# Softmax sums of a dilated attention kernel: the [112, 4, 12] tile of sums and reciprocals moves from SBUF to the PSUM bank of the scores

## The chip, the cores and the metric

The kernel runs on one core of one Trainium2 chip. The metric is device time in microseconds (us) of one execution. Three runs of the kernel before gave 5148.28, 5153.74 and 5155.06 us; their median, 5153.74 us, is the time that the change is compared with.

## What is computed

The input x has shape (16, 56, 56, 384) in float32: 16 images of 56 x 56 pixels with 384 channels. Two layers are applied, each as x + f(group_norm(x)) with 32 groups of 12 channels. The first f is an attention over the 3 x 3 neighbours of each pixel, for three groups of 128 channels with dilations 1, 2 and 3, and 4 heads of 32 channels in each. The second is a 3 x 3 depthwise convolution with weights clipped and replaced by their sign. Cut to what matters:

```python
qkv = einsum('bchw,oc->bohw', group_norm(x), w_qkv)     # 3 x 384 outputs
for each dilation group, head and pixel:
    attn = einsum('bgdn,bgdkn->bgnk', q, k_of_9_neighbours) * 32 ** -0.5
    attn = softmax(attn, axis=-1)                       # over the 9 neighbours
    out  = einsum('bgnk,bgdkn->bgnd', attn, v_of_9_neighbours)
x = x + einsum('bhwc,oc->bhwo', out, w_proj) + b_proj
x = x + depthwise_conv3x3(group_norm(x), sign(clip(w_conv)))
```

The change sits in the softmax: in the sums over the nine neighbours, their reciprocals and the product with them.

## The kernel before, in words

The work is cut into strips of 8 image rows (448 pixels); an image has 7 of them, so there are 112, which are numbered 0 to 111 here. Channels lie on the partitions, pixels along the free dimension. Three plans put the pieces of a strip at due times: `plan_a` brings the input in, transposes it (`turn`, L435) and takes statistics (L448); `plan_b` does the attention; `plan_c` does the second normalisation (L721, L789), the convolution (L752, L762 to L768 for two of the three channel groups; L818, L825 and L831 to L834 for the third) and the transposes back for the output (L841). `plan_b` starts a strip every 9 steps, and `plan_c` handles the strip of ten strips earlier, so that some sixteen strips are in flight.

The attention of one strip goes like this.

- `k_or_v` and `query` project the normalised input with matmuls (L476) into PSUM tiles `pkv` and `pq`. ScalarE copies k and v to SBUF (L486).
- `score` multiplies `pq` with k shifted to three neighbours at a time, on VectorE (L529, nine instructions of 1344 elements for each strip).
- `score_rounds` sums the products over the 32 channels of each head with matmuls (L514) into one PSUM tile `ps`, which collects all 27 pairs of group and neighbour. They are issued in three bursts of 8, 8 and 11 matmuls, the first after the third L529 of its strip.
- `softmax_1` copies `ps` to SBUF (ScalarE, L544), transposes it so that pixels lie on 112 partitions (L547, tile `pt_s`), takes the maximum over the neighbours (L550, tile `mx`), subtracts it (L551) and applies the exponential (ScalarE, L552). The weights are in the SBUF tile `ew`, 4 x 108 elements on 112 partitions.
- `softmax_2` sums the weights over the neighbours (L556), takes the reciprocals (L557) and multiplies (L558), all on VectorE. The tile in between, `sm`, holds 48 elements on each partition.
- `softmax_3` to `softmax_5` split the weights into three bf16 terms (ScalarE L566, GpSimd L570, L574, L575), and a DMA transposes them (L580).
- `weigh` spreads the weights over the channels with small matmuls (L593, tile `pb_a`), multiplies them with v on VectorE (L600) and adds up on GpSimd (L608, 1344 elements; L611 and L612).
- `out_project` projects (L626, tile `po`) and adds bias and residual (L629).

What sets the order: each piece is put at a step and, within a step, at a rank (`at(when, order, piece)`); sorted by these, the pieces give the program order. In step 9m + 10 of strip m `softmax_2` comes first. The first score burst of strip m + 1 is due at step 9m + 11. A scheduler then orders the instructions of each engine by its own estimates of cost, and puts in the waits on semaphores. [...]

Tiles come from pools. A pool with n buffers for a tag gives a buffer to the next tile of that tag when every instruction that used the tile before has finished. [...]`ps_mt` has three (most matmul outputs), `ps_q` one, `ps_bc` three in one tile (`pb_a`), and `ps_s` has the last, with a single tile tag "s" and one buffer. Before the change only `ps` (L508) used it. `sm` shares the tag "mx" with `mx` in the SBUF pool `s_p`, also with one buffer.

The kernel before has these three places around the change:

```python
had["ps"] = ps_s.tile([P, 512], F32, tag="s", name="ps")          # L508
at(t0 + 10, SOFTMAX, softmax_2)                                    # L648
at(t0 + i, BURST, lambda i=i: score_rounds(3 if i == 8 else 2))    # L646
```

Of the kernel before, what the change touches and what calls it, by code (L numbers as in the profile page):

```python
# [8 lines left out]
F32 = mybir.dt.float32  # L9
# [8 lines left out]
P = 128  # L18
# [6 lines left out]
SUB = 112  # L25
# [10 lines left out]
def dilated_attention_then_binary_conv(  # L36
# [32 lines left out]
    NSUB = PX // SUB  # L69
# [17 lines left out]
    ps_s = ctx.enter_context(tc.tile_pool(name="ps_s", bufs=1, space=PSUM))  # L87
# [67 lines left out]
    s_p = ctx.enter_context(tc.tile_pool(name="s_p", bufs=1))  # L155
# [302 lines left out]
    def plan_b(m, t0):  # L458
# [73 lines left out]
        GH = NG * HEADS  # L532
        weights = ew.rearrange("p (s v) -> p s v", s=NSUB)[:, :, :NR]

        def by_neighbour(ap):
            return ap.rearrange("p s (o k) -> p s o k", o=NTAP)

        def over_neighbours(ap):
            return ap.unsqueeze(2).to_broadcast([SUB, NSUB, NTAP, GH])
# [12 lines left out]
            nc.scalar.activation(weights, weights, AF.Exp, scale=SCALE)  # L552

        def softmax_2():
            sm = s_p.tile([SUB, NSUB, GH], F32, tag="mx", name="sm")
            nc.vector.reduce_sum(sm, by_neighbour(weights).rearrange("p s o k -> p s k o"), axis=AX.X)  # L556
            nc.vector.reciprocal(sm, sm)  # L557
            nc.vector.tensor_tensor(by_neighbour(weights), by_neighbour(weights), over_neighbours(sm), ALU.mult)  # L558
# [84 lines left out]
        for i in range(9):  # L643
            at(t0 + i, SCORE, lambda i=i: score(i))
            if i % 3 == 2:
                at(t0 + i, BURST, lambda i=i: score_rounds(3 if i == 8 else 2))  # L646
        at(t0 + 9, SOFTMAX, softmax_1)
        at(t0 + 10, SOFTMAX, softmax_2)  # L648
        at(t0 + 11, SOFTMAX, softmax_3)
        at(t0 + 11, SOFTMAX, softmax_4)  # L650
# [318 lines left out]
```

## Time and profile before

| what | value |
|---|---|
| median of three runs | 5153.74 us |
| the profiled execution's own time | 5160.07 us |
| its span, first to last instruction | 5157.9 us |
| mean granted TensorE clock | 0.979 |
| TensorE (PE) busy | 96% |
| VectorE (DVE) busy | 87% |
| GpSimd (POOL) busy | 82% |
| ScalarE (ACT) busy | 48% |
| DMA over the span | 162 GB/s mean |
| instructions | 72661 |

How to read it: the page and the answers of the trace come from one execution, which took 5160.07 us, 0.12% more than the median of the runs. In a list of groups each line has the line of the kernel, the engine, the operation, output and inputs, the shape, the count, then busy time in us, mean duration in ns, and the idle time of the engine just before with what ended it. In a timeline each line has the start in us from the beginning of the span, the duration in us, engine, line and operation; a bracket at the end gives the idle time before it and what ended it. A float32 matmul shows as two records, so a burst of 8 matmuls is "x16". The clock column PEclk is the share of full TensorE clock that was granted.

### The profile page before, as it was taken

How to read it: one execution, taken by the hardware profiler on the slowest of the kernel's cores; microseconds unless marked ns; L12 is line 12 of the kernel's file. 1: busy time of each engine (PE TensorE's matmuls, PEld its weight loads, DVE VectorE, ACT ScalarE, POOL GpSimd, SP SyncE). 2: the span in 40 equal slices, each digit the busy share in tenths (PEclk: the TensorE clock that was granted, in tenths of full speed). 3: DMA queues.
4: the chain of work that ended last, by engine and by line, in shares of the span. 5: the costliest groups of instructions: out<-in, count | busy, mean ns of one | idle time of the engine just before them, and what ended most of it. 6: DMA issues, size and time to landing. Idle time of an engine off the chain costs nothing. (4 is left out here: it accounts for less than half of the span.)

```text
span 5157.9 us, 72661 instructions
## 1 busy us (share of the span) xinstructions
PE 4967.5 (96%) x25093; PEld 2259.1 (44%) x25093; DVE 4475.9 (87%) x4575; ACT 2478.8 (48%) x4365; POOL 4248.0 (82%) x2998
## 2 busy tenths in 40 slices
PE   7999999999999999999999999999999999999975
PEld 4444444444444444444444444444444444444422
DVE  4888888888898888898888898888889988888876
ACT  3223545555454555545545554554555545444445
POOL 2778888888888888889888888888889888888891
PEclk8999999999999999999999999999999999999986
DMA  6443666666566665666666666666656656555455
GB/s 194 125 123 112 171 170 175 171 168 172 166 172 167 169 169 167 172 163 172 170 175 169 168 174 169 168 168 167 173 164 174 168 166 170 146 135 139 119 144 162
DMA packets 813957, 836.45 MB, mean 162 GB/s; under 512 B 362643, under 2 KB 782870, under 8 KB 813590
## 3 DMA queue, kind: packets, MB, share of 16 engines
q1 hardware_dynamic: 805606, 819.81, 57.8%
q10 hardware_dynamic: 7984, 12.00, 0.7%
q8 instruction: 199, 3.26, 0.3%
q14 instruction: 168, 1.38, 0.1%
HBM read 477.43 MB, written 231.21 MB: 137 GB/s over the span
## 5 line engine op out<-in xcount | busy, mean ns | idle before, releaser
L608 POOL TENSOR_TENSOR w<-w 128x1344 f32<-128x1344 f32 x672 | 2049.5, 3050 | 300.8 <-DVE w L600 262.3
L600 DVE TENSOR_TENSOR w<-pb_a,v 128x1344 f32<-128x1344 f32 x1008 | 1561.6, 1549 | 132.5 <-PE pb_a L593 102.1
L529 DVE TENSOR_TENSOR t<-pq,k 128x1344 f32<-128x1344 f32 x1008 | 1527.6, 1547 | 130.0 <-PE pq L476 128.8
L476 PE MATMUL pkv<-xn,wqkvT 128*128 128x448 f32 x3924 | 1553.3, 545 | 26.7 <-ACT xa L447 26.2
L476 PEld LDWEIGHTS pkv<-xn,wqkvT 128*128 128x128 f32 x3924 | 727.6, 191 | 706.4 <-issue 631.6
L476 PE MATMUL pq<-xn,wqkvT 128*128 128x448 f32 x1962 | 862.4, 567 | 0.0
L626 PE MATMUL po<-y,wprojT 128*128 128x448 f32 x2016 | 836.2, 551 | 20.1 <-POOL y L612 17.3
L721 ACT ACTIVATE z<-z,mrz 96x448 f32<-96x448 f32 x840 | 580.4, 752 | 262.6 <-DMA z<-x1d 220.6
L825 POOL TENSOR_TENSOR m<-m 128x1344 f32<-128x1344 f32 x210 | 640.0, 3047 | 68.6 <-ACT m L818 62.6
L514 PE MATMUL ps<-t,sel 128*32 128x448 f32 x6048 | 661.1, 546 | 1.8 <-DVE t L529 1.7
L818 ACT ACTIVATE m<-zg,ktap 128x448 f32<-128x448 f32 x945 | 568.9, 659 | 17.6 <-POOL m L825 8.5
L626 PEld LDWEIGHTS po<-y,wprojT 128*128 128x128 f32 x2016 | 375.8, 191 | 378.8 <-issue 346.2
L486 ACT COPY v<-pkv 128x448 f32<-128x448 f32 x336 | 178.5, 531 | 755.2 <-PE pkv L476 755.1
L476 PEld LDWEIGHTS pq<-xn,wqkvT 128*128 128x128 f32 x1962 | 339.4, 190 | 349.9 <-issue 349.9
L593 PE MATMUL pb_a<-aT,spread 24*128 24x448 bf16 x3024 | 370.4, 360 | 52.6 <-DVE w L600 48.4
L629 DVE SCALAR_TENSOR_TENSOR xr<-po,bias,xr 128x448 f32<-128x448 f32 x336 | 227.5, 677 | 210.7 <-PE po L626 205.8
L612 POOL TENSOR_TENSOR y<-y,w 128x448 f32<-128x448 f32 x336 | 381.7, 1136 | 20.3
L611 POOL TENSOR_TENSOR y<-w 128x448 f32<-128x448 f32 x336 | 382.3, 1138 | 17.3
L447 ACT COPY xa<-pt_x 128x448 f32<-128x448 f32 x315 | 167.4, 533 | 474.6 <-PE pt_x L435 469.2
L593 PEld LDWEIGHTS <-spread 24*128 24x128 bf16 x3024 | 102.5, 91 | 627.5 <-issue 608.6
L570 POOL TENSOR_TENSOR rest<-ew,e 112x512 f32<-112x512 f32 x112 | 130.2, 1163 | 292.5 <-ACT e L566 291.3
L752 PE MATMUL pc<-z,kdiag 96*32 96x440 f32 x3360 | 359.5, 546 | 8.8 <-POOL z L723 7.6
(141 smaller groups left out, 4745.8 us busy)
## 6 DMA issues: line engine op xcount, KB each, us to landing
z<-x1d SPq DMA_DIRECT2D x570, 224.0 KB, 3.8
xr<-xd SPq DMA_DIRECT2D x112, 672.0 KB, 4.3
x1d<-xr SPq DMA_DIRECT2D x112, 672.0 KB, 3.2
xn<-xd SPq DMA_DIRECT2D x109, 672.0 KB, 4.6
xin<-in_x_dram SPq DMA_DIRECT2D x105, 672.0 KB, 7.8
xd<-xa SPq DMA_DIRECT2D x315, 224.0 KB, 3.6
out_dram<-osb SPq DMA_DIRECT2D x420, 168.0 KB, 3.5
x<-x1d SPq DMA_DIRECT2D x80, 560.0 KB, 5.7
```

What stands on the lines that cost most here:

```text
L476: nc.tensor.matmul(dst[:, :PX], wqkvT[:, cc, o0 : o0 + P], had["xn"][:, cc, :], start=(cc == 0), stop=(cc == NG - 1))
L514: return nc.tensor.matmul(had["ps"][32 * j : 32 * j + 32, :PX], sel[:, s0 : s0 + 32], tk, start=(issued[j] == 1), stop=(issued[j] == len(r ...
L529: nc.vector.tensor_tensor(t.rearrange("p k (r w) -> p k r w", w=W), q3, k3, ALU.mult)
L593: return nc.tensor.matmul(pb[:, kx, :PX].rearrange("p (s n) -> p s n", s=NSUB), spread[rows_of, v % 2, :], had["a"][rows_of, :, v // 8, :] ...
L600: nc.vector.tensor_tensor(w.rearrange("p k (r w) -> p k r w", w=W), pb[:, :, :PX].rearrange("p k (r w) -> p k r w", w=W), three(kv[1][g][m ...
L608: nc.gpsimd.tensor_tensor(w0, w0, w, ALU.add)
L611: nc.gpsimd.tensor_tensor(y, w0[:, 0], w0[:, 1], ALU.add)
L612: nc.gpsimd.tensor_tensor(y, y, w0[:, 2], ALU.add)
L626: nc.tensor.matmul(po[:, :PX], wprojT[:, g, j * P : (j + 1) * P], had[f"y{g}"], start=(g == 0), stop=(g == NG - 1))
L721: nc.scalar.activation(z, z, AF.Identity, bias=mrz[:, j, q, 0:1], scale=mrz[:, j, q, 1:2])
L818: nc.scalar.activation(rows(t[:, kx]), zp[:, ky : ky + ROWS, kx : kx + W], AF.Copy, scale=ktap[:, JG, o : o + 1])
L825: nc.gpsimd.tensor_tensor(had["m"], had["m"], t, ALU.add)
```

## The change

In `softmax_2` the tile `sm` is no longer taken from the SBUF pool `s_p` (tag "mx") but from the PSUM pool `ps_s` with the tag "s", the one buffer that `ps` uses. The first 48 columns of 112 partitions of that bank hold the sums and then their reciprocals. The three VectorE instructions stay, with the same shapes; the sum now writes PSUM, the reciprocal reads and writes PSUM, and the product reads its second operand from PSUM. Every later line of the file moves down by one.

```diff
         def softmax_2():
-            sm = s_p.tile([SUB, NSUB, GH], F32, tag="mx", name="sm")
+            sm = ps_s.tile([P, 512], F32, tag="s", name="psm")[:SUB, : NSUB * GH]
+            sm = sm.rearrange("p (s k) -> p s k", s=NSUB)
             nc.vector.reduce_sum(sm, by_neighbour(weights).rearrange("p s o k -> p s k o"), axis=AX.X)
             nc.vector.reciprocal(sm, sm)
             nc.vector.tensor_tensor(by_neighbour(weights), by_neighbour(weights), over_neighbours(sm), ALU.mult)
```

In the built program the tag now passes from `ps` of strip m to `psm` of strip m and on to `ps` of strip m + 1. The order of instructions on each engine is the same for most of the span. On TensorE it differs in two stretches. For strips 3 to 9 one of the three L476 matmuls for `pq` that stood behind the first score burst stands ahead of it. In the last image, for most strips, the eight L752 matmuls that stood behind the first score burst stand ahead of it; with them a few L600, L762, L765 and L768 change places on VectorE.

## The prediction

> **What bounds the kernel now.** I read the page first, then the groups of VectorE by form, then the timeline around L558 in single strips, then the waits of TensorE by stretch.
>
> The page's first part:
>
> ```profile
> PE 4967.5 (96%) x25093; PEld 2259.1 (44%) x25093; DVE 4475.9 (87%) x4575; ACT 2478.8 (48%) x4365; POOL 4248.0 (82%) x2998
> ```
>
> TensorE sets the pace: in strips 10 to 99 one L558 follows another after 43.40 us again and again, and the matmuls follow each other without gaps. Whatever delays TensorE there lengthens the run one for one; VectorE time alone is worth nothing. So the question is where this change touches TensorE. The groups of VectorE by form (count, then busy us and mean ns) show the three instructions concerned and their nearest relatives:
>
> ```profile
> L558 DVE TENSOR_TENSOR ew<-ew,sm 112x432 f32<-112x432 f32 x112 | 118.2, 1055 | 3.7
> L556 DVE TENSOR_REDUCE sm<-ew 112x48 f32<-112x432 f32 x112 | 102.1, 911 | 0.2 <-ACT ew L552 0.2
> ...
> L551 DVE TENSOR_TENSOR ew<-pt_s,mx 112x432 f32<-112x432 f32 x112 | 65.9, 589 | 0.0
> L557 DVE RECIPROCAL sm<-sm 112x48 f32<-112x48 f32 x112 | 50.7, 452 | 3.7
> ```
>
> L558 and L551 do the same work on the same shape, yet L558 takes 1055 ns on average and L551 589. The tile view of `sm` gives L558 as 586/608/3077 ns (minimum, median, maximum): most are normal and some are stopped. The timeline of such a strip:
>
> ```profile
> 2363.94 0.91 DVE L556 TENSOR_REDUCE sm<-ew 112x48 f32<-112x432 f32 x1
> 2364.22 3.06 POOL L608 TENSOR_TENSOR w<-w 128x1344 f32<-128x1344 f32 x1
> ...
> 2364.89 0.45 DVE L557 RECIPROCAL sm<-sm 112x48 f32<-112x48 f32 x1
> ...
> 2365.38 2.38 DVE L558 TENSOR_TENSOR ew<-ew,sm 112x432 f32<-112x432 f32 x1
> ...
> 2365.97 1.71 PE L514 MATMUL ps<-t,sel 128*32 128x448 f32 x16
> ...
> 2369.80 0.37 PE L593 MATMUL pb_a<-aT,spread 24*128 24x448 bf16 x3 [0.64 <-DVE w L600]
> ```
>
> L558 (start 2365.38) ends at 2367.76, half a microsecond after GpSimd's L608 ends (2367.28). L556 and L557 run at normal length beside the same L608. L600, two instructions behind L558, is late, its bank is late, and TensorE stands still for 0.64 us before L593. In a strip where L608 is out of the way:
>
> ```profile
> 2539.17 0.45 DVE L557 RECIPROCAL sm<-sm 112x48 f32<-112x48 f32 x1
> ...
> 2539.66 0.61 DVE L558 TENSOR_TENSOR ew<-ew,sm 112x432 f32<-112x432 f32 x1
> ...
> 2540.25 1.71 PE L514 MATMUL ps<-t,sel 128*32 128x448 f32 x16
> ```
>
> L558 takes 0.61 us and ends at 2540.27. The score burst starts at 2540.25: free of L558 now, but at the same moment by chance. That coincidence matters below.
>
> [...]L558 has two SBUF inputs and stalls up to 3077 ns; L551 with one input in PSUM has a longest duration of 608 ns in 112.[...]
>
> **The change part by part.** I numbered the 112 instances of L558 in order of time and noted the TensorE gap after each.
>
> 1. [...]After the change L558 has one SBUF input, as L551 has, so I take all stalls away (0 to 100% is the range; it is a rival below). In strips 10 to 99 29 of 90 are stalled, 31.8 us together. A stall costs TensorE nothing up to an L558 of about 1.67 us, since L593 has 1.06 us of slack behind L600; beyond that one for one (1.96 us gives 0.29, 2.38 us gives 0.71). Only 15 strips pay, 8.8 us in all. That is 28% of the stall time; the rest was hidden behind the matmuls of L514 and L752 anyway. Gain: 8.8.
>
> 2. The last image (strips 100 to 110). VectorE is fuller there and nine L558 stall, by 13.6 us. The waits of TensorE in the window 4480 to 4940:
>
> ```profile
> PE pb_a L593 <- DVE w L600: 13.5, 9, 2.5
> ```
>
> After four of these waits the granted clock reads 0.50, for 3.4, 6.8, 6.8 and 10.2 us (4530.2, 4574.6, 4707.7 and 4844.3 on), 27.2 us together, so 13.6 us of work are lost, about 2 of them inside the waits. The ceiling is 13.5 + 11.5 = 25 us. But strips 100 and 107, which do not stall, take 43.43 and 43.34 us to the next, as long as strips 103 and 104 that wait for 1.7 us (43.23 and 43.35): they wait 0.8 us at L626 for ScalarE's L486 instead. So most of a wait comes back. I credit 0.4 us for each of nine waits (3.6) and 70% of the clock loss (8): 12, with 3 to 22 as ends. In the new order L752 stands ahead of the burst (1.54 us of matmuls), which covers the new wait here.
>
> 3. Added: the wait of the first score burst for L558. Behind it on TensorE stand L752, L593 and all else of the strip; VectorE's L762 and L600 wait for those. A TensorE instruction that waits for VectorE starts 0.055 us after its end (the floor of L593 after L600 and of L514 after L529). In 78 of the 90 strips the burst starts 0.01 us before the end of an unstalled L558, so it moves by 0.065 us: 5.1 us. In the other 12 it starts 0.07 us after it: nothing. The 0.065 us repeats in each strip, since the chain L529 to L558 is itself started by TensorE (`pq`): no slack takes it up.
>
> 4. Strips 3 to 9: the burst started 0.80 us before the end of L558 (306.08 against 306.88). One L476 now stands ahead of it, two records 0.375 us apart, 0.75 us. What is left is 0.80 + 0.055 - 0.75, about 0.1 us, seven times: 0.7.
>
> 5. The three instructions with a PSUM operand. Product: L551 (one PSUM input) is 19 ns shorter than an unstalled L558. Writing PSUM: L762 takes 687 ns to PSUM, L629 677 to SBUF: +10 for L556. Reciprocal: no such row. [...]I take 0. Each 0.01 us is worth 0.9 us.
>
> 6. The very last strip stalls by 2.5 us with little to cover it, and the rest of its attention hangs on it; I credit 1.
>
> Sum: -8.8 - 12 - 1 + 5.1 + 0.7 + 0 = -16.0 us. From the profiled 5160.07 that gives 5144.1, or -0.31%; from the median, 5153.74, about **5138 us**.
>
> If the cover in 1 is wrong the gain only grows. If the cover in 2 (L752 ahead of the burst) fails, the burst waits 0.46 us there, 11 times: 5 us back.
>
> **The rivals.**
>
> Absorbed (chance 0.25): the new wait eats the gain. The last image gives back all but 3 us, and the chain grows by 0.05 us: -16 + 9 + 4.5 = -2.5, 5151 us. For it: strips 100 and 107[...]. Against it: the halved clock disappears with the waits that come before it.
>
> Longer chain (0.08, slower): the reciprocal on PSUM, whose cost no row shows, makes the chain x longer; every burst waits it out, some 100 strips, 100 x x. It cancels the gain at x = 0.16 us and counts as slower (+10 us) from x = 0.26. At 0.4 us: -16 + 40 = +24, 5178 us. Against it: L551, L600 and L529 read PSUM at about the speed at which others read SBUF.
>
> [...] (0.05, slower): the change would not do what it says, because the product still reads and writes `ew` in SBUF. Then a stalled L558 holds the burst itself: 31.8 + 5.1 instead of 8.8 in strips 10 to 99, +28, 5182 us. It decides when about half of the stall time is left. Against it: L551 writes the same tile and never stalls.
>
> Forecast: 0.62.
>
> **How the numbers follow.** About 0.2% (10 us) is what a measurement of this kernel can tell from no change. The forecast's own range is 5126 (last image at its ceiling, shorter chain) to 5148; nearly all of it is faster (0.60 of 0.62). Of the absorbed case 0.03 counts as faster, 0.22 as the same. Faster 0.63, same 0.24, slower 0.13. The range reaches from 5124, with about 0.05 below, to 5155, which takes in the absorbed case and leaves out the two slower ones.
>
> **What would show it.** The product (then L559) at about 590 ns with no instance over 700;[...] L514 starting 0.05 to 0.06 us after the product's end in most strips, with 43.47 us from strip to strip; no wait of L593 on L600 at this place; no half clock between 4500 and 4930. The prediction is wrong if the product still has stalls, if the chain of three is longer by over 0.15 us, or if the strips of the last image are as long as before.

## The result, and the profile after

| | median us | runs | range us |
|---|---|---|---|
| before | 5152.51 | 4 | 5148.28 to 5155.06 |
| after | 5123.98 | 4 | 5119.31 to 5126.29 |

The ratio is 0.9944, with a 95% interval of 0.9927 to 0.9962: faster by 28.5 us. The forecast was 5138, its range ended at 5124. The direction was right; the gain was about half of what came. The profiled execution after took 5122.06 us (span 5120.0, mean granted clock 0.985 against 0.979).

The first part of the page after has this line for the engines:

```profile
PE 4945.2 (97%) x25093; PEld 2247.6 (44%) x25093; DVE 4427.5 (86%) x4575; ACT 2479.0 (48%) x4365; POOL 4247.7 (83%) x2998
```

TensorE is still the bound. VectorE is 48.4 us less busy, and that is the work of one group, the product (118.2 us before, 67.5 after). The groups of VectorE by form (count, then busy us and mean ns; the lines have moved down by one):

```profile
L557 DVE TENSOR_REDUCE psm<-ew 112x48 f32<-112x432 f32 x112 | 102.9, 919 | 0.2 <-ACT ew L552 0.2
L559 DVE TENSOR_TENSOR ew<-ew,psm 112x432 f32<-112x432 f32 x112 | 67.5, 603 | 3.6
...
L551 DVE TENSOR_TENSOR ew<-pt_s,mx 112x432 f32<-112x432 f32 x112 | 65.9, 589 | 0.0
L558 DVE RECIPROCAL psm<-psm 112x48 f32<-112x48 f32 x112 | 52.1, 466 | 3.7
```

The product went from 1055 to 603 ns on average, the sum from 911 to 919, the reciprocal from 452 to 466. The tile view of `psm` shows that no product is stopped any more (minimum, median, maximum), and who waits for the tile instead (PEld is the weight load of a matmul):

```profile
L559 DVE TENSOR_TENSOR ew<-ew,psm x112: 577/603/606, 110.5 to 4942.2; 112x432 f32<-112x432 f32 x112
...
who waited for it (us, times):
  PEld ps L514: 30.1, 101
```

The strip of 2365.38 that the prediction showed, in the timeline after (start, us, engine):

```profile
2361.59 3.08 POOL L609 TENSOR_TENSOR w<-w 128x1344 f32<-128x1344 f32 x1
...
2362.35 0.47 DVE L558 RECIPROCAL psm<-psm 112x48 f32<-112x48 f32 x1
...
2362.85 0.60 DVE L559 TENSOR_TENSOR ew<-ew,psm 112x432 f32<-112x432 f32 x1
...
2363.51 1.71 PE L514 MATMUL ps<-t,sel 128*32 128x448 f32 x16
...
2366.64 0.36 PE L594 MATMUL pb_a<-aT,spread 24*128 24x448 bf16 x3
```

GpSimd's L609 runs from 2361.59 to 2364.67, so the product starts and ends inside it, at full speed. This holds throughout. Before, 40 products were stalled; all of them start while an L608 runs, and each ends 0.46 to 0.47 us after that L608 does. After, 50 products start while an L609 runs, and none takes over 606 ns. The burst starts 0.06 us after the product's end (2363.45), the new wait; L594 has no wait in brackets.

So much is as forecast. The gain is not where the forecast had put it. I numbered the products in order of time in both traces and compared the stretches between them. "The last image" stands for the stretch from product 99 on, as in the prediction. With seven strips to an image these are the last strips of the last but one image and all of the last; `plan_a` has no input left to transpose there (its last L435 is at 4402 us in the kernel before).

| stretch | before us | after us | difference | forecast |
|---|---|---|---|---|
| product 3 to 10 | 287.8 | 288.0 | +0.2 | +0.7 |
| product 10 to 99 | 3915.0 | 3912.7 | -2.3 | -3.7 |
| product 99 to 111 (last image) | 543.1 | 514.4 | -28.7 | -12 |
| product 111 to the end | 182.8 | 177.8 | -5.0 | -1 |

The remaining 2.1 us lie ahead of product 3. The two profiled executions are 38.0 us apart and the medians 28.5, since the profiled one of before was over 7 us above its median; the last image is nevertheless the term to explain. The waits of TensorE there, in the kernel after from 4440 to 4940 (us, times, longest):

```profile
PE po L627 <- ACT v L486: 4.3, 3, 2.0
PE pb_a L594 <- DMA aT<-e: 3.7, 1, 3.7
PE ps L514 <- DVE t L529: 1.7, 1, 1.7
PE pv L350 <- POOL dev L344: 1.5, 2, 0.9
PE pb_a L594 <- DVE w L601: 1.1, 2, 0.7
```

The 13.5 us of waits of the `pb_a` matmuls (L593 before, L594 after; the expectations below call them bias matmuls) for VectorE are down to 1.1.

### The profile page after: what moved, and what is told of

Read it like the earlier page. It is cut to its first block, busy times and chain, and to the rows that moved or that the text cites. A ratio compares the mean times of both kernels' runs of the same rounds, so it can differ in the third digit from the quotient of the medians.

```text
span 5120.0 us, 72665 instructions
## 1 busy us (share of the span) xinstructions
PE 4945.2 (97%) x25093; PEld 2247.6 (44%) x25093; DVE 4427.5 (86%) x4575; ACT 2479.0 (48%) x4365; POOL 4247.7 (83%) x2998
## 3 DMA queue, kind: packets, MB, share of 16 engines
q14 instruction: 168, 1.38, 0.1%
## 5 line engine op out<-in xcount | busy, mean ns | idle before, releaser
L609 POOL TENSOR_TENSOR w<-w 128x1344 f32<-128x1344 f32 x672 | 2049.7, 3050 | 301.7 <-DVE w L601 258.8
L601 DVE TENSOR_TENSOR w<-pb_a,v 128x1344 f32<-128x1344 f32 x1008 | 1561.6, 1549 | 125.9 <-PE pb_a L594 95.2
L529 DVE TENSOR_TENSOR t<-pq,k 128x1344 f32<-128x1344 f32 x1008 | 1528.3, 1547 | 125.8 <-PE pq L476 124.6
L476 PE MATMUL pkv<-xn,wqkvT 128*128 128x448 f32 x3924 | 1545.4, 543 | 23.2 <-ACT xa L447 22.7
L476 PEld LDWEIGHTS pkv<-xn,wqkvT 128*128 128x128 f32 x3924 | 724.3, 190 | 698.2 <-issue 628.7
L476 PE MATMUL pq<-xn,wqkvT 128*128 128x448 f32 x1962 | 854.1, 562 | 0.0
L627 PE MATMUL po<-y,wprojT 128*128 128x448 f32 x2016 | 835.0, 550 | 18.8 <-POOL y L613 14.1
L514 PE MATMUL ps<-t,sel 128*32 128x448 f32 x6048 | 662.9, 548 | 4.6 <-DVE t L529 2.4
L486 ACT COPY v<-pkv 128x448 f32<-128x448 f32 x336 | 178.5, 531 | 746.0 <-PE pkv L476 745.6
L476 PEld LDWEIGHTS pq<-xn,wqkvT 128*128 128x128 f32 x1962 | 337.0, 189 | 341.9 <-issue 340.7
L594 PE MATMUL pb_a<-aT,spread 24*128 24x448 bf16 x3024 | 368.8, 359 | 32.1 <-DVE w L601 26.7
L753 PE MATMUL pc<-z,kdiag 96*32 96x440 f32 x3360 | 356.3, 542 | 9.5 <-POOL z L724 8.2
L594 PEld LDWEIGHTS <-spread 24*128 24x128 bf16 x3024 | 100.0, 91 | 603.7 <-issue 584.1
L486 ACT COPY k<-pkv 128x448 f32<-128x448 f32 x336 | 178.4, 531 | 357.3 <-PE pkv L476 357.3
```

The source lines that it names most:

```text
L476: nc.tensor.matmul(dst[:, :PX], wqkvT[:, cc, o0 : o0 + P], had["xn"][:, cc, :], start=(cc == 0), stop=(cc == NG - 1))
L514: return nc.tensor.matmul(had["ps"][32 * j : 32 * j + 32, :PX], sel[:, s0 : s0 + 32], tk, start=(issued[j] == 1), stop=(issued[j] == len(r ...
L529: nc.vector.tensor_tensor(t.rearrange("p k (r w) -> p k r w", w=W), q3, k3, ALU.mult)
L594: return nc.tensor.matmul(pb[:, kx, :PX].rearrange("p (s n) -> p s n", s=NSUB), spread[rows_of, v % 2, :], had["a"][rows_of, :, v // 8, :] ...
L601: nc.vector.tensor_tensor(w.rearrange("p k (r w) -> p k r w", w=W), pb[:, :, :PX].rearrange("p k (r w) -> p k r w", w=W), three(kv[1][g][m ...
L609: nc.gpsimd.tensor_tensor(w0, w0, w, ALU.add)
```

## The experiments

The theory after the result (A): in the last image every wait behind a stalled product, and the half clock after it (stretches in which the granted clock reads 0.50), came back in full. The rivals: the excess lies in the other hundred strips (D); or it is the new order of TensorE's instructions in the last image that brought it, not the end of the stalls (B). For after has the depthwise convolution's first matmuls (L753) ahead of the score burst there, before had the burst ahead and `pb_a` right behind it.

### The two halves of the kernel

```diff
-            sm = s_p.tile([SUB, NSUB, GH], F32, tag="mx", name="sm")
+            if m >= 99:
+                sm = ps_s.tile([P, 512], F32, tag="s", name="psm")[:SUB, : NSUB * GH]
+                sm = sm.rearrange("p (s k) -> p s k", s=NSUB)
+            else:
+                sm = s_p.tile([SUB, NSUB, GH], F32, tag="mx", name="sm")
```

The diff is that of e_last; e_first has `m < 99` in its place. In these and the other kernels the lines behind the edit are moved down by a few; the tiles name the instructions. PSUM only from strip 99 on:

> PSUM tile for the sums only from strip 99 on, SBUF tile before. Theory A (in the last image the waits of TensorE behind the stalled products and the half clock after them come back in full, about 25 to 29 us, against the 12 of step 2): 24 to 30 us under the kernel before, about as much as the whole change less 3. Theory D (step 2's 12 was right, and the excess lies in the other hundred strips): 10 to 14 us under the kernel before. In the profile of this run the stalled products are gone from strip 99 on and still there in strips 10 to 98, at 43.40 us from strip to strip.

PSUM only up to strip 98:

> The complement: PSUM tile only up to strip 98, SBUF tile from 99 on. Theory A: the strips 10 to 98 give 8.8 us of stalls and lose some 78 x 0.08 = 6.2 to the new wait, strips 3 to 9 lose 1: 1 to 4 us under the kernel before, and the waits of the first bias matmul (line 593 of the kernel before) and the half clock in the last image are still there. Theory D: 14 to 18 us under.

The kernel after, beside them on the same chip:

> The kernel after, for the comparison with its parts on the same chip: 26 to 31 us under before. Theory A: equal to the sum of the two halves (last image, and the rest) within 3 us.

Before was 5151.94 us here (25 runs).

| kernel | median us | against before | ratio, 95% interval |
|---|---|---|---|
| e_last | 5127.44 | -24.5 | 0.9953 (0.9940 to 0.9965) |
| e_first | 5146.25 | -5.7 | 0.9988 (0.9982 to 0.9995) |
| after | 5124.70 | -27.2 | 0.9948 (0.9935 to 0.9960) |

D falls: thirteen of 112 strips hold 24.5 of 27.2 us. The two halves add up to 30.2, 3.0 more than the whole, within what the intervals allow (that of e_last alone runs from 18 to 31 us). e_first gained a little more than expected; its strips 10 to 99 took 3912.5 us, the 2.6 less than before that the table above also shows.

### The kernel before, profiled once more

> The kernel before, profiled once more, to see how far the half clock behind the waits of the last image differs between executions. Its profiled execution took 5160.07 us, 7.5 over its median, and had lost 20.5 us to the half clock between the products of strips 99 and 111; a run with the same tiles in these strips (PSUM up to strip 98 only) had lost 11.9 there. If the half clock is what differs, this execution is near 5152 us with 10 to 14 us lost there, and the same nine waits, 13 to 16 us together.

5151.46 us, so the 5160 was high (the 25 runs of before above go from 5146.58 to 5164.03), but the half clock was not the reason, against what I had expected: 18.8 us were lost to it between products 99 and 111 and the stretch took 541.1 us. The difference to the first profile was in the start and the end (178.4 against 182.8 us after product 111). A second profile of after (e_after) gave 521.0 us for the last image, 6.5 more than the first, because a projection waited 5.1 us for ScalarE's L486. The means of two profiles each, 542.1 and 517.7, differ by 24.4 us, and that is also the 24.5 of e_last's median. I take 24.5, not 28.7, for what the last image was worth; e_last's figure has the tail in it.

Not all of this comes from stalled products. Strip 99 took 48.42 and 46.74 us in the two profiles of before and 44.50 and 44.51 in those of after, though its product is not stalled in any of them. In before `pb_a` waits there 22 us behind the product:

```profile
4454.03 0.37 PE L593 MATMUL pb_a<-aT,spread 24*128 24x448 bf16 x3 [2.37 <-DVE w L600]
```

In after this wait is 0.39 us: the weighting that it waits for stands ahead of two convolution instructions on VectorE (L766 and L769), where before it stood behind them (L765 and L768). Two kernels with the SBUF tile and its stalls, but in an order that an edit changed (e_sbuf_pc1 and e_wait, below), also take 44.51 us for strip 99. So 2 to 4 us of the last image belong to the order of instructions and not to the stalls.

### Where the last image was blocked: order or stall

Under A the end of the stalls alone brings the gain of the last image. The burst put back ahead of the convolution there, PSUM tile as in after (an order between instructions without a wait; `burst_mm[m]` holds the matmuls of strip m's first burst, and the lines that fill it are left out here and in the next diff):

```diff
+                if j == 0 and (kx, q) == (0, 3) and 100 <= m + 10 <= 111:
+                    tc.add_manual_dep(mm.ins, burst_mm[m + 10][-1].ins.name, mybir.DependencyInfo(
+                        mybir.DependencyClass.NoSync, mybir.DependencyReason.DATA))
```

> PSUM tile everywhere as in the kernel after, but in the last image the first score burst is put ahead of the depthwise convolution's matmuls (L753 of the kernel after), as in the order before. Theory A ([...]the order only covers the new wait): the burst waits some 0.5 us for the product in 11 strips, 3 to 7 us over the kernel after, 20 to 24 under before, no half clock between 4500 and 4930. Theory B (a good part of the gain of the last image comes from the new order): 12 to 18 us over the kernel after.

The SBUF tile with the convolution put ahead of the burst:

```diff
+                if j == 0 and (kx, q) == (2, 2) and 100 <= m + 10 <= 111 and m % NCH:
+                    tc.add_manual_dep(burst_mm[m + 10][0].ins, mm.ins.name, mybir.DependencyInfo(
+                        mybir.DependencyClass.NoSync, mybir.DependencyReason.DATA))
```

> SBUF tile as before, but in the last image the depthwise convolution's first matmuls stand ahead of the first score burst, as in the order after. Theory A: the products stall as before, the bias matmul waits as before and the clock is halved as before: within 5 us of the kernel before. Theory B: 10 to 17 us under it.

Half of the change, sums in PSUM and reciprocals in SBUF:

```diff
-            nc.vector.reciprocal(sm, sm)
+            psm, sm = sm, s_p.tile([SUB, NSUB, GH], F32, tag="mx", name="sm")
+            nc.vector.reciprocal(sm, psm)
```

> Only half of the change: the sums are reduced into PSUM, but their reciprocals go to an SBUF tile, so the product has two SBUF inputs again, and the score bank is free after the reciprocal. If the second SBUF input of the product is what made it stall, the stalls are all there (an average product over 1000 ns) and no burst waits for the product: within 6 us of the kernel before. If it were the sums in SBUF (the reduction or the reciprocal) that mattered: 20 to 30 us under it.

The other half, sums in SBUF and reciprocals in PSUM:

```diff
-            nc.vector.reduce_sum(sm, by_neighbour(weights).rearrange("p s o k -> p s k o"), axis=AX.X)
-            nc.vector.reciprocal(sm, sm)
+            ssm = s_p.tile([SUB, NSUB, GH], F32, tag="mx", name="sm")
+            nc.vector.reduce_sum(ssm, by_neighbour(weights).rearrange("p s o k -> p s k o"), axis=AX.X)
+            nc.vector.reciprocal(sm, ssm)
```

> The other half of the change: the sums stay in an SBUF tile, only the reciprocals are written to the PSUM tile, so the product has one SBUF input. If that input alone decides, no product stalls, the burst waits for the product as in the kernel after, and the time is that of the kernel after within 4 us (24 to 30 us under before), 43.46 to 43.48 us from strip to strip. If the place of the sums mattered too, part of the stalls or of the waits stays: 5 to 20 us under before.

Before was 5150.54 us beside the first three (41 runs), 5149.13 beside the last (9 runs). The last two columns are from each kernel's trace.

| kernel | median us | against before | ratio, 95% interval | stalls in strips 100 to 110, us | product 99 to 111, us |
|---|---|---|---|---|---|
| e_psum_burst1 | 5130.62 | -19.9 | 0.9962 (0.9948 to 0.9975) | 0 | 508.6 |
| e_sbuf_pc1 | 5146.45 | -4.1 | 0.9988 (0.9982 to 0.9995) | 11.2 | 530.2 |
| e_recip_sbuf | 5140.10 | -10.4 | 0.9979 (0.9972 to 0.9985) | 12.2 | 520.9 |
| e_sum_sbuf | 5125.65 | -23.5 | 0.9953 (0.9940 to 0.9967) | 0 | 510.8 |

e_sum_sbuf has the time of after within the noise (23.5 us under before, just short of the 24 to 30 expected), and its product takes the same 603 ns. In e_recip_sbuf the sums are in PSUM, but the product has two SBUF inputs again and stalls again. So the product's second operand alone decides whether it stalls. The groups of VectorE of e_sum_sbuf, then the tile view of `sm` in e_recip_sbuf:

```profile
L560 DVE TENSOR_TENSOR ew<-ew,psm 112x432 f32<-112x432 f32 x112 | 67.5, 603 | 3.7
```

```profile
L560 DVE TENSOR_TENSOR ew<-ew,sm x112: 586/608/3342, 110.5 to 4953.3; 112x432 f32<-112x432 f32 x112
```

e_psum_burst1 and e_sbuf_pc1 came out in the bands of A or at their edge: stalls removed and order not as in after, most of the gain; order changed and stalls still there, next to nothing. Of the 4.1 us of e_sbuf_pc1, strip 99 alone can be 2 to 4. But e_psum_burst1 has its number for another reason than expected. In it the scheduler put one of the matmuls for `pq` (two records, 0.85 us) ahead of the burst, so the eleven waits of 0.5 us did not come: its strips in the last image are as short as those of after (41.58 us). The 5.9 us that its median lies above that of e_after is in no stretch that I could pin down: between product 99 and the end it took 696.3 us, the two profiles of after 692.2 and 696.7.

And e_recip_sbuf missed: I expected it within 6 us of before, and it is 10.4 faster although its products stall as before. The reason is in the timelines of one strip of the last image, number 103. The kernel before:

```profile
4616.07 2.00 DVE L558 TENSOR_TENSOR ew<-ew,sm 112x432 f32<-112x432 f32 x1
...
4616.29 1.71 PE L514 MATMUL ps<-t,sel 128*32 128x448 f32 x16
...
4617.99 1.54 DVE L600 TENSOR_TENSOR w<-pb_a,v 128x1344 f32<-128x1344 f32 x1
...
4619.59 0.37 PE L593 MATMUL pb_a<-aT,spread 24*128 24x448 bf16 x3 [1.59 <-DVE w L600]
...
4619.88 1.68 PE L752 MATMUL pc<-z,kdiag 96*32 96x440 f32 x16
```

The kernel after:

```profile
4599.07 0.60 DVE L559 TENSOR_TENSOR ew<-ew,psm 112x432 f32<-112x432 f32 x1
...
4599.26 1.69 PE L753 MATMUL pc<-z,kdiag 96*32 96x440 f32 x16
...
4599.59 1.55 DVE L601 TENSOR_TENSOR w<-pb_a,v 128x1344 f32<-128x1344 f32 x1
...
4600.76 1.69 PE L514 MATMUL ps<-t,sel 128*32 128x448 f32 x16
...
4602.38 0.36 PE L594 MATMUL pb_a<-aT,spread 24*128 24x448 bf16 x3
```

e_recip_sbuf:

```profile
4609.89 2.90 DVE L560 TENSOR_TENSOR ew<-ew,sm 112x432 f32<-112x432 f32 x1
...
4610.08 1.71 PE L514 MATMUL ps<-t,sel 128*32 128x448 f32 x16
...
4611.61 1.66 PE L754 MATMUL pc<-z,kdiag 96*32 96x440 f32 x16
...
4612.71 1.54 DVE L602 TENSOR_TENSOR w<-pb_a,v 128x1344 f32<-128x1344 f32 x1
...
4614.31 0.37 PE L595 MATMUL pb_a<-aT,spread 24*128 24x448 bf16 x3 [1.03 <-DVE w L602]
```

Read it as a race between two engines from the product on. VectorE needs the product, then one weighting (L600, 1.54 us), then 0.055 us to wake TensorE. Before, TensorE has only the burst to do in that time. The product took 2.00 us instead of 0.61; without these 1.39 us the chain would have let `pb_a` start at 4619.59 - 1.39 = 4618.20. The burst was done 1.59 us before L593, at 4618.00. So `pb_a` is late by 0.2 us even without a stall, and strips 100 and 107, which have none, show exactly that (0.21 and 0.20 us). There is no cover here at all: a stall of 1.39 us gives a wait of 1.59. In e_recip_sbuf the burst and the convolution both lie ahead of `pb_a`: a stall of 2.90 - 0.61 = 2.29 us gives a wait of 1.03, one of 1.73 in the next strip 0.47, so 1.26 us are covered. In after both lie ahead too: L601 ends at 4601.14, `pb_a` starts at 4602.38, some 1.2 us after it could have.

So the last image had two cures, and after took both: no stall, and the cover. Take the six strips with the long waits, 101 to 105 and 108: 274.3 us before, 249.7 after.

- e_psum_burst1 has no stall and the convolution behind `pb_a`, and takes 249.7 too. So the convolution's cover is not needed. It is not the order of before, though: the `pq` matmul ahead of the burst leaves 0.45 us of slack (in strip 103 the weighting ends at 4605.56 and `pb_a` starts at 4606.07). In the order of before some 0.2 us a strip would be left by the sum above; that was not run.
- e_recip_sbuf has the cover, and stalls of 0.70 to 2.29 us in five of these strips (1.37 to 2.33 us in all six before), and takes 250.8. So the cover brings nearly all of it there without the first cure. Why its median is all the same 15 us above that of after is not settled: in its profile strip 99 keeps its long wait (48.43 us), strips 100 and 107 wait 3.8 and 2.7 us for ScalarE's L486, and the time from product 111 on is 186.5 us.
- e_sbuf_pc1 shows why merely turning two groups round did little: there `pb_a` slipped in between convolution and burst, with one group of eight matmuls ahead of it as before and 12.3 us of waits.

An SBUF tile in after's own order was not run.

### The price of the new wait

The wait alone, with the SBUF tile and its stalls, which is the prediction's rival of +28 us; the first matmul of each strip's first burst waits for the product of the strip before (`product[m]` is the product of strip m, noted in `softmax_2`; the lines around are left out):

```diff
+            def add_first(a):
+                done = issued[a[0] % NQ] == 0 and sum(issued) == 0 and m - 1 in product
+                mm = add(*a)
+                if done:
+                    tc.add_manual_dep(mm.ins, product[m - 1].ins.name, mybir.DependencyInfo(
+                        mybir.DependencyClass.Sync, mybir.DependencyReason.DATA))
+                return mm
```

> SBUF tile as before, so the stalls stay, with the wait alone added by hand: the first matmul of each strip's first score burst waits for the product of the strip before. [...]Theory A (a stalled product now holds the burst itself, and each 0.1 us on this path is paid once per strip): strips 10 to 98 pay all 31.7 us of stalls in place of the 8.5 that they paid, and 78 x 0.08 us for the wait, 29 us more than before; with strips 3 to 9 some 30 us over the kernel before; in the last image two matmul pairs and the first bias matmul stand ahead of the burst, and it stays within 5 us of before. Rival: the stall is partly taken up further on, as it was before; 5 to 15 us over the kernel before.

5177.13 us against 5150.54: 26.6 slower (ratio 1.0050, 1.0036 to 1.0064). Strips 10 to 99 took 3945.0 us, 30.0 more than before. The waits of TensorE from 499 to 4439, and the strip of 2365.38 once more:

```profile
PE ps L515 <- DVE ew L567: 26.5, 22, 1.7
```

```profile
2378.00 2.32 DVE L567 TENSOR_TENSOR ew<-ew,sm 112x432 f32<-112x432 f32 x1
...
2380.38 1.71 PE L515 MATMUL ps<-t,sel 128*32 128x448 f32 x16 [1.71 <-DVE ew L567]
```

Every stall is now paid by the burst: the 22 stalled products stall by 26.8 us, the 22 waits last 26.5. What stands behind the burst on TensorE is held back with it: strips with a wait of 1.71 us are 45.18 us long, those without a wait 43.46. Four of the waits, of some 1.7 us, are also followed by half clock of 3.4 us, 6.8 us lost in all; in before no such stretch lies between products 10 and 99. The prediction's rival had its sum of 28 us without this term, and with 31.8 us of stalls where 26.8 came, so that it is so near to 30.0 is in part luck. It failed because the stalls went, not because the new wait is cheap. The last image was not within 5 us of before: at 530.4 us it is 11.7 shorter than the mean of the two profiles of before, with strip 99 short, no stall in strip 101 and less half clock (10.2 us lost).

PSUM only where the stalls were (`NCH` is 7, so it is one strip in seven, not in eight as the expectation says: 14 of them, and the 13 from 99 on):

```diff
+            if m % NCH == 3 or m >= 99:
+                sm = ps_s.tile([P, 512], F32, tag="s", name="psm")[:SUB, : NSUB * GH]
+                sm = sm.rearrange("p (s k) -> p s k", s=NSUB)
```

> PSUM tile only in the strips in which the product was often stalled (one in eight, and all from strip 99 on), SBUF tile elsewhere. If the new wait costs 0.08 us in each steady strip, as the two profiles say (43.475 against 43.395 us), some 65 strips get it back: 4 to 7 us under the kernel after, 32 to 36 under before, with 43.40 us between the strips that have the SBUF tile. Rival: in those strips the stalls that stay cost as much as the wait, or the product meets the GpSimd instruction at other strips as the phase moves: within 2 us of the kernel after.

5119.16 us (5117.52 to 5121.11), 32.8 under before (ratio 0.9938, 0.9925 to 0.9952) and 5.5 under after, the fastest of all. Strips 10 to 99 took 3907.6 us, 5.1 less than in after. The tile view of its `psm` (now 27 instances) shows who still waits:

```profile
  PEld ps L514: 6.0, 17
```

17 bursts wait instead of 101. The remaining SBUF products stall by 9.1 us in strips 10 to 99; the waits of `pb_a` for VectorE there are 13.5 us against 14.8 in after, so what is left of the stalls is covered but for 0.4 us in one strip.

## Why the prediction was right about the change and wrong about its size

- **Step 1, the stalls of the product (8.8).** Right. All 29 stalls are gone (products of up to 3077 ns in before, at most 606 in after; what in L608 holds a product with two SBUF inputs was not shown), and the net of strips 10 to 99 is -2.3 us in the first pair of profiles and -2.6 in e_first. With the wait of step 3 at its measured 0.08 us, 78 x 0.08 = 6.2, the removed stalls were worth 8.5 to 8.8.
- **Step 2, the last image (12).** This is the step that failed. Its argument was that "most of a wait comes back", because strips 100 and 107, without a stall, were as long as 103 and 104 with one. That comparison was of unlike strips. Without its waits strip 100 takes 43.43 - 0.83 - 0.21 = 42.39 us and strip 107 takes 43.34 - 0.75 - 0.20 = 42.39; strip 103 takes 43.23 - 1.59 = 41.64. In after, 103 takes 41.59, while 100 and 107 stay at 43.63 and 44.32 with waits of 1.30 and 2.00 for L486. Strips 100 and 107 were long for reasons of their own (0.8 us more, which I did not trace further, and 1.0 us of waits), and I read this as the length that a strip returns to. In the strips with the long waits every wait came back whole, and so did the clock. In strips 101 to 105 and 108 the waits of L593 were 11.5 us and the half clock cost 13.6, together 25.1; these six strips became 274.3 - 249.7 = 24.6 us shorter. In the second pair of profiles the sum is 11.0 + 6.8 = 17.8, and they became 267.5 - 249.8 = 17.7 us shorter. The ceiling of 25 in the prediction lies near all this (e_last measured 24.5, with the tail), but in part by luck: it left out strip 99, it counted 0.4 us of waits in strips 100 and 107, and it took about 2 us of the half clock to lie inside the waits, while TensorE was busy in 27.01 of those 27.20 us.
- **L752 ahead of the burst.** It was taken as cover for the new wait. It also gives `pb_a` some 1.2 us of slack where before it was late by 0.2. The prediction did not see this second effect.
- **Step 3, the new wait (0.065 us in 78 strips).** Right in kind, a little small: 0.08 us from strip to strip (43.475 against 43.395). The burst went from 0.012 us before the product's end to 0.055 after it, 0.067 against the 0.065 forecast; the rest is about what the chain of step 5 grew by. e_select gets 5.1 us back by not paying it in most strips.
- **Step 4, strips 3 to 9 (0.7).** Twice as much: 38.56 us a strip became 38.75 in strips 3 to 7, and with strip 8 it is 1.3 us. The burst now starts 0.13 us after the product's end, later than the floor of 0.055 that the prediction put there. Strip 9 hides this in the table of stretches: in the two profiles of before it took 53.03 and 51.36 us. e_last and e_select, with SBUF tiles there, take 286.2 and 286.4 us for this stretch, after and e_first 288.0.
- **Step 5, the chain of three (0).** It grew by 8 + 14 - 5 = 17 ns, counted against an unstalled product of 608 ns. No larger price of PSUM shows: the reciprocal is 14 ns longer from PSUM to PSUM, and 4 ns from PSUM to SBUF (457 in e_recip_sbuf); the product is 5 ns shorter. L600 and L529, which the prediction sets against the rival "longer chain", read `pb_a` and `pq` in PSUM and took 1549 and 1547 ns for 1344 elements in before, 1.15 ns an element, where the unstalled product took 608 ns for 432 from SBUF, 1.41. That rival went with these numbers.
- **Step 6, the tail (1).** Between -2.7 and -5 us by the profiles, but this stretch differs by 4 us between two executions of one kernel (182.8 and 178.4 before). Not settled.

Of the signs that the prediction named, the product (at most 606 ns), the start of L514 (0.055 us after the product) and the 43.475 us from strip to strip held; "no half clock between 4500 and 4930" held to 4910, where a wait of 3.69 us for a DMA starts that of the last strips; in the second profile of after there was one more, behind the 5.1 us at the projection.

## What to carry to other kernels

When an engine at its bound waits now and then, subtract the traced waits and the half clock from the strips that have them and compare what is left; don't take another strip's length for the length without a wait before its own waits are subtracted. Then follow the race from the late instruction to the wait on both engines: how much work of the waiting engine lies between them says how much of a stall is paid (nothing of the first 1.06 us in the steady strips, all of it in the last image of the kernel before), and here a reordering took away nearly as much of the wait as the end of the stall did (250.8 against 249.7 us in six strips). And where a buffer's new place costs a wait in every round and helps in some, give it only to those: e_select is 5.5 us faster than the whole change.

## What the runs showed that I had not expected

The granted clock was halved after waits of some 1.6 us, and not after each of them. In the kernel before the waits of 1.64 us (at 4573.11) and 1.57 us (at 4706.14) are followed by this (window, busy us of each engine, then PEclk):

```profile
4574.60:4581.40 6.80, 6.80 (x20) 2.58 (x13) 4.36 (x6) 0.00 (x0) 6.72 (x5) 0.50 0.30 56
...
4707.70:4714.50 6.80, 6.80 (x21) 2.74 (x14) 4.43 (x6) 0.00 (x0) 6.58 (x6) 0.50 0.31 58
```

while the waits of 1.59 and 1.69 us between them are not. TensorE was busy all through these 6.8 us, at half speed (from 4577.66 to 4580.07 an L476 starts every 0.75 to 0.91 us, from 4581.45 on every 0.376), so each costs 3.4 us, twice its wait. In the traces of before and after the half-clock stretches between products 3 and 111 last 3.4, 6.8 or 10.2 us, and which waits are followed by one differs between executions of the same kernel: in the second profile of before strip 103 has it, whose wait is 1.6 us too, and 102 and 105 don't. So a short wait on TensorE has a price that the list of waits doesn't show, and it has to be read from the granted clock.

The traces say a little more. The changes of the granted clock lie on a grid of 3.413 us in each trace. Cut the time from product 3 to 111 into the windows of this grid, in all twelve traces, and take the windows at full clock: all 43 with 2.0 us or more of idle TensorE were followed by half clock, and none of the 134 that had between 1.0 and 1.38 us, so the waits of 1.2 us in the steady strips never were. Of the 60 in between 27 were. The wait of 1.59 us in strip 103 is divided by the grid, with 0.98 us in the fuller window, which fits that no half clock follows. But the 1.69 us of strip 104 lie inside one window, like the 1.57 and the 1.64, and aren't followed by it either. What decides between 1.4 and 2.0 us stays open.
